# A new order behind the last attention steps: layer-norm statistics, Newton steps, scalings and gates

## The chip, the cores and the metric

The kernel runs on one core of a Trainium2 chip. The metric is the device time in microseconds (us), the median of several runs; less is better. A profile is one execution, in which the hardware profiler records every instruction of each engine. The engines are named as in the profile: PE (matrix multiplication; PEld are its weight loads), DVE (vector), ACT (activation), POOL (GpSimd), SP (which here only issues transfers). Each engine works through its own queue in order; an instruction that waits holds up all behind it on that engine.

## The reference

Sixteen batches `x[b]` of 128 tokens with 512 features go through cross-attention and then through a mixture of experts, each with a layer norm in front and a residual add behind:

```python
x = x + xattn(layernorm(x), ctx, ctx)      # 32 query heads of 16, 8 key heads, 128 context tokens
h = layernorm(x)
scores = sigmoid(h @ gate_weight.T)        # 32 experts in 8 groups
# the best 4 groups by the sum of their two best, then the 8 best experts, weights normed, times 2.5
x = x + sum of the 8 weighted experts(h) + shared expert(h)   # expert: (silu(h w1) * (h w3)) w2
```

All is float32.

## The kernel before

The order of the instructions on PE, DVE, ACT and POOL is written by hand: each engine gets them in the order in which the Python code calls them. SP's transfers stand in the order of their calls too. Waits between engines follow from the data and from buffers that are used again.

Attention (`attention_small`) is a loop over 32 items `(b, i)`, two for each batch. At step n it calls what the dictionary `head` holds for n, then `scores` of item n (PE, then exponentials on ACT, L481), `values` and `add` of item n - 1, `gates` at some steps, what `middle` holds, transposes of the next batch's queries at even steps, transposes of normed rows at some steps, and what `tail` holds.

The parts that matter here:

- `values` (PE L489) fills a PSUM bank, and DVE transposes it out (L499). `add` divides on DVE (L512, L514) and adds to `x[b]` on POOL (L521). For the last batch, 15, each half is added by itself, the second one on DVE.
- `layernorm_stats(b, SECOND)` (DVE L95, L96) takes mean and variance of the rows of `x[b]` after attention. `layernorm_rstd(first, n)` makes 1/sqrt for n batches in Newton steps: twelve tiny instructions on POOL (L102 to L132) or nine on DVE (L102 to L120).
- `gate_rows(b)` scales the rows to the normed `xn` (L136; on DVE or POOL) and has SP write them to `rows` in DRAM (L235). The tile has four buffers.
- `turn_of(b)` ("turn" below): four PE transposes of `xn` (L451) into a bank, which ACT copies to `xall` (L527); for batch 14 DVE copies. `queries(b)` does the same with query rows `xq` (scaled on DVE, L136; copied on ACT, L462).
- `gates(b)`: the gate logits of batches b and b + 1 (PE L540) into a bank, and their transpose by DVE into `logits` (L548).
- All these small products (`values`, turns, queries, gates) share two PSUM banks (`one_bank`, tag `m`) in turn, so each waits until the one before the last is evicted.
- `filler(n)`: n matmuls of the shared expert (PE L285, two records each), which need only batches 0 to 3 and can stand anywhere.

Behind the loop a hand-written tail finishes values, turns 11 to 15 and the gates 8, 10, 12 and 14. Then `route` picks the experts: sigmoid on ACT, a long chain on DVE up to `sel` (L1184) with 21 more fillers on PE, and the counting matmuls (L1192). Then come the slot tables, and the experts, which take the time from about 204 us on. POOL has, behind its part of the tail, a row of memsets (L1014 to L1027) that prepare the experts.

`turned[n]` says which batch is turned at step n, `parts[n]` which gates run at step n (n = 16, 20, 24 and 28 for batches 0, 2, 4 and 6). Statistics of batch b < 14 stand in `tail` at step 2b + 4. POOL's Newton steps run for batches 12 and 13 (columns 28 and 29) in `head` at step 31, and DVE's for 14 and 15 in the tail.

Of the kernel before, what the change touches and what calls it, by code (L numbers as in the profile page):

```python
# [46 lines left out]
def tile_xattn_moe(  # L47
# [15 lines left out]
    nc = tc.nc  # L63
# [29 lines left out]
    def layernorm_stats(b, norm):  # L93
        st = xnp.tile([P, 6], F32, tag="st", name="st")
        nc.vector.bn_stats(st, xs[b])  # L95
        nc.vector.bn_aggr(mv[:, norm[b], :], st)  # L96
# [37 lines left out]
    def normalized(out, of, b, norm, eng=nc.vector):  # L134
        n = norm[b]
        eng.tensor_scalar(out, of, mv[:, n, 0:1], rstd[:, n : n + 1], ALU.subtract, ALU.mult)  # L136
# [19 lines left out]
    SECOND = [*range(12, 15), *range(18, 21), *range(22, 2 * B)]  # L156
# [75 lines left out]
    def gate_rows(b, eng):  # L232
        xn = xnp.tile([P, D], F32, tag="xn2", name="xn2", bufs=4)
        normalized(xn, xs[b], b, SECOND, eng)
        nc.sync.dma_start(rows[ts(b, P), 0:D], xn)  # L235
        xn2[b] = xn
# [67 lines left out]
    def attention_small():  # L304


        with ExitStack() as ph:
# [6 lines left out]
            def one_bank(n=TB):  # L314
                return ps_m.tile([P, TB], F32, tag="m", name="m")[:, 0:n]
# [38 lines left out]
            def keep_warm(n):  # L354
                warm = one_bank(P) if n else None
                for _ in range(n):
                    nc.tensor.matmul(warm, lhsT=wz, rhs=wz, start=True, stop=True)
# [85 lines left out]
            def transposes(of, permuted, then):  # L443
                x = one_bank()
                for k in range(4):
                    if permuted:
                        to = x.rearrange("p (q g s) -> p g q s", g=4, s=HP)[:, k]
                        by = ident.rearrange("p (q s) -> p q s", s=HP)
                    else:
                        to, by = x[:, ts(k, P)], ident  # L450
                    nc.tensor.matmul(  # L451
                        to, lhsT=of[:, k, :], rhs=by, start=True, stop=True, is_transpose=True
                    )
                then(x)

            def queries(b):

                xn = xqs.pop(b).rearrange("p g k d -> p g (k d)")

                def then(x):  # L460
                    qTs[b] = ap2.tile([P, TB], F32, tag="qT", name="qT")
                    (nc.scalar.copy if b > 1 else nc.vector.tensor_copy)(qTs[b], x)  # L462

                return xn, True, then
# [19 lines left out]
            def values(b, i):  # L484
                oT = one_bank()
                for j in range(NJ):
                    p = ps.pop((b, i, j))
                    for q in range(P // HP):
                        nc.tensor.matmul(  # L489
                            oT[q * HP : (q + 1) * HP, ts(j, P)],  # L490
                            lhsT=vas[b // 4 % 2][:, b % 4, 2 * j + i, :],
                            rhs=p[:, ts(q, P)],
                            start=True,
                            stop=True,
                            tile_position=(0, q * HP),
                        )
                if i == 0:
                    os[b] = ap2.tile([P, 2, NJ * G, HP], F32, tag="o", name="o")
                nc.vector.transpose(os[b][:, i].rearrange("p h e -> p (h e)"), oT)  # L499

            def add(b, i, eng=nc.gpsimd):

                if b < B - 1:
                    if i == 0:
                        return
                    both = slice(0, 2)
                else:
                    both = slice(i, i + 1)
                n = both.stop - both.start
                o = os[b][:, both]  # L510
                ri = ap2.tile([P, 2, NJ * G], F32, tag="ri", name="ri")[:, 0:n]
                nc.vector.reciprocal(ri, o[:, :, :, HD])  # L512
                at = ap2.tile([P, 2, NJ * G, HD], F32, tag="at", name="at")[:, 0:n]
                nc.vector.tensor_tensor(  # L514
                    at,
                    o[:, :, :, 0:HD],
                    ri.unsqueeze(3).to_broadcast([P, n, NJ * G, HD]),
                    ALU.mult,
                )
                part = xs[b].rearrange("p (j i e) -> p i j e", i=2, e=G * HD)[:, both]  # L520
                eng.tensor_tensor(  # L521
                    part, part, at.rearrange("p i (j g) d -> p i j (g d)", g=G), ALU.add
                )

            def turn_of(b, copy=nc.scalar.copy):
                def then(x):
                    copy(  # L527
                        xnT[b // 4][:, :, ts(b % 4, P)], x.rearrange("p (k s) -> p k s", s=P)
                    )

                return xn2.pop(b).rearrange("p (k d) -> p k d", d=P), False, then
# [3 lines left out]
            def gates(b):  # L535
                lgT = one_bank(2 * E)
                of = xnT[b // 4].rearrange("p d (n q t) -> p d q n t", n=4, t=E)
                for k in range(ND):
                    for q in range(P // E):
                        nc.tensor.matmul(  # L540
                            lgT[q * E : (q + 1) * E].rearrange("p (n t) -> p n t", t=E),
                            lhsT=gw[:, k, :],
                            rhs=of[:, k, q, b % 4 : b % 4 + 2],
                            start=(k == 0),
                            stop=(k == ND - 1),
                            tile_position=(0, q * E),
                        )
                nc.vector.transpose(logits[:, b : b + 2, :].rearrange("p n e -> p (n e)"), lgT)  # L548
# [3 lines left out]
            head, middle, tail = {}, {}, {}  # L552

            def at(where, n, f, *a):
                where.setdefault(n, []).append((f, a))
# [33 lines left out]

            turned, parts = {}, {}  # L590
            for b in range(14):
                at(tail, 2 * b + 4, layernorm_stats, b, SECOND)
            for n, group in ((10, (8, 7)), (16, (15, 6)), (22, (21, 4)), (27, (25, 3))):
                at(head, n, layernorm_rstd, *group, nc.gpsimd)
            at(head, 31, layernorm_rstd, 28, 2, nc.gpsimd)
            for b in range(11):
                n = min(2 * b + 13, b + 21)
                turned[n] = b
# [10 lines left out]
            for n in range(N):  # L609
                for f, a in head.get(n, ()):  # L610
                    f(*a)

                scores(*items[n])
                if n == 1:
                    transposes(*queries(1))
                if n > 0:
                    values(*items[n - 1])
                    add(*items[n - 1])
                if n in parts:
                    gates(parts[n])  # L620
                for f, a in middle.get(n, ()):
                    f(*a)
                if n % 2 == 0 and 0 < n // 2 < B - 1:
                    transposes(*queries(n // 2 + 1))
                if n in turned:
                    transposes(*turn_of(turned[n]))
                keep_warm(FILL.get(n, 0))
                for f, a in tail.get(n, ()):
                    f(*a)

            gate_rows(12, nc.gpsimd)
            nc.scalar.activation(table, table, AF.Sigmoid)
            gu = ps_sc.tile([P, 2, TB], F32, tag="sc", name="gu")
            banks = iter([gu[:, i] for i in range(2)])
# [3 lines left out]
            def filler(n):  # L640
                for _ in range(n):
                    next(matmuls)

            filler(1)
            values(*items[N - 1])
            add(*items[N - 1], nc.vector)
            transposes(*turn_of(11))
            gate_rows(13, nc.gpsimd)
            gates(8)
            layernorm_stats(14, SECOND)  # L650
            layernorm_stats(15, SECOND)
            layernorm_rstd(SECOND[14], 2)
            filler(1)
            gates(10)
            filler(2)
            transposes(*turn_of(12))
            transposes(*turn_of(13))
            filler(1)
            gates(12)
            gate_rows(15, nc.vector)  # L660
            transposes(*turn_of(15))
            gate_rows(14, nc.vector)
            transposes(*turn_of(14, nc.vector.tensor_copy))
            gates(14)
            filler(3)
# [1356 lines left out]

    pieces = [(k, i) for k in range(NTB) for i in range(NI)]
    left_over = attention_small()
    experts(pieces[1:], in_order, *left_over)
    left = nc.values_load(
# [64 lines left out]
```

## Time and profile before

| | us |
|---|---|
| median of 3 runs | 855.24 (854.67 to 856.40) |
| profiled execution | 855.98 |
| its span, first to last instruction | 853.80 |
| PE busy | 830.5 (97%) |
| DVE busy | 686.4 (80%) |
| ACT busy | 670.9 (79%) |
| POOL busy | 479.3 (56%) |
| first scores matmul of attention | 9.1 |
| last values matmul of attention | 100.7 |
| gates(14) on PE | 112.76 to 113.41 |
| counting matmuls of routing | from 134.14 |

The times in a row of the timeline are the start from the beginning of the span and the length; brackets hold the engine's idle time in front and what ended it. The granted TensorE clock was 0.997 of full speed over the span.

### The profile page before, as it was taken

The page shows a single profiled execution, that of the slowest core. Times are in us where ns is not written, and L with a number is a line of the kernel's source. Part 1 is how long each engine was busy: PE and PEld are TensorE (multiplying, and loading weights), DVE is VectorE, ACT ScalarE, POOL GpSimd, SP SyncE. Part 2 cuts the span into 40 slices and gives each one's busy share as a digit, 9 for nine tenths or more (in the row PEclk, how much of TensorE's full clock was granted, in tenths as well). Part 3 has the DMA queues.
Part 4 walks back from the last instruction along what each step waited for, and adds up shares of the span by engine and source line. Part 5 has one row for each costly group of instructions (what it writes and reads, how often), then busy time and mean ns, then how long its engine had stood idle before and what let it go on. Part 6 is the DMA issues. An engine that isn't in the chain of part 4 may idle for free.

```text
span 853.8 us, 14954 instructions
## 1 busy us (share of the span) xinstructions
PE 830.5 (97%) x4847; PEld 604.2 (71%) x4847; DVE 686.4 (80%) x1660; ACT 670.9 (79%) x1225; POOL 479.3 (56%) x574
## 2 busy tenths in 40 slices
PE   8999989999999999999999999999999999999995
PEld 6555544546676866777787878687878899887763
DVE  7987878849887977988898989898979999986210
ACT  5989622538988896988988989888888999998631
POOL 4597640053445676465548565766657666655453
PEclk9999999999999999999999999999999999999998
DMA  9211113456666798577769696978787978785653
GB/s 282 94 51 64 50 40 128 169 158 197 185 151 150 170 188 240 134 193 174 190 150 234 157 238 157 214 169 199 177 197 187 211 192 188 181 216 126 93 83 50
DMA packets 59879, 137.23 MB, mean 161 GB/s; under 512 B 12168, under 2 KB 16392, under 8 KB 59792
## 3 DMA queue, kind: packets, MB, share of 16 engines
q0 software_dynamic: 32032, 69.25, 41.1%
q1 hardware_dynamic: 27680, 66.81, 23.5%
q8 instruction: 40, 0.66, 0.3%
q14 instruction: 47, 0.39, 0.1%
q10 hardware_dynamic: 80, 0.13, 0.1%
HBM read 96.71 MB, written 46.73 MB: 168 GB/s over the span
## 4 chain that ended last, share of the span: by engine, by line
PE 78%; DVE 7%; ACT 6%; issue 4%; DMA 2%; POOL 2%; POOLq 0%; DVEq 0%; ACTq 0%
PE p L1540 39%; PE y L1781 15%; PE gu L285 6%; PE y L1681 6%; ACT xall L1435 4%; PE y L1334 3%; PE m L489 2%; POOL out_dram L1653 2%; PE sc L471 2%; DMA out_dram<-yp,token 2%; PE gu L1470 2%; PE m L451 2%; DVE o L499 1%; DVE st L95 1%; PE tok L985 1%
## 5 line engine op out<-in xcount | busy, mean ns | idle before, releaser
L1435 ACT COPY xall<-blocks 32x512 f32<-32x512 f32 (+4 forms) x684 | 360.4, 527 | 10.9 <-DVE blocks L1438 0.9
L1653 POOL DMA_INDIRECT out_dram<-yp,token x122 | 201.2, 1649 | 153.6 <-ACT yp L1793 43.2
L1397 POOL DMA_INDIRECT xgs<-rows,token x138 | 153.3, 1111 | 126.1 <-DVE token L997 59.9
L1540 PE MATMUL p<-xall,wup 128*128 128x270 f32 (+27 forms) x720 | 185.9, 393 | 0.0
L1540 PEld LDWEIGHTS p<-xall,wup 128*128 128x128 f32 x720 | 136.7, 190 | 31.6 <-issue 4.7
L1540 PE MATMUL p<-t,s 128*128 128x270 f32 (+27 forms) x480 | 123.6, 394 | 0.0
L1540 PEld LDWEIGHTS p<-t,s 128*128 128x128 f32 x480 | 91.1, 190 | 20.2 <-issue 3.2
L1438 DVE STREAM_TRANSPOSE blocks<-xgs 128x512 f32<-128x512 f32 x138 | 97.0, 703 | 0.0
L1681 PE MATMUL y<-wdn,sa 128*32 128x512 f32 (+2 forms) x288 | 78.7, 596 | 0.0
L1653 POOL DMA_INDIRECT out_dram<-yw,token x28 | 45.1, 1609 | 51.2 <-DMA out_dram<-yw,token 26.1
L481 ACT ACTIVATE p<-sc 128x1024 f32<-128x1024 f32 x64 | 62.0, 1024 | 6.8 <-PE sc L471 6.1
L1550 DVE TENSOR_TENSOR z<-u,p 128x270 f32<-128x270 f32 (+27 forms) x96 | 48.4, 504 | 22.0 <-PE p L1540 21.9
L1540 PE MATMUL p<-xall,s 128*128 128x270 f32 (+27 forms) x240 | 63.5, 395 | 0.8 <-DVE z L1550 0.8
L1540 PE MATMUL p<-t,wup 128*128 128x270 f32 (+27 forms) x240 | 63.8, 396 | 0.0
L285 PE MATMUL gu<-xall,sup 128*128 128x512 f32 x128 | 58.8, 600 | 0.0
L1793 ACT ACTIVATE yp<-yp,wt 128x256 f32<-128x256 f32 (+1 forms) x96 | 54.3, 608 | 3.7 <-DVE yp L1772 2.6
L1772 DVE TENSOR_TENSOR yp<-sdn,y 128x512 f32<-128x512 f32 x72 | 49.1, 682 | 9.7 <-PE y L1781 4.7
L1540 PEld LDWEIGHTS p<-t,wup 128*128 128x128 f32 x240 | 44.9, 190 | 14.7 <-DVE z L1550 3.7
L1540 PEld LDWEIGHTS p<-xall,s 128*128 128x128 f32 x240 | 45.2, 190 | 14.1 <-issue 3.9
L1781 PE MATMUL y<-sup,sa 128*128 128x256 f32 x192 | 49.9, 382 | 3.2 <-ACT sdn L1836 3.0
L1681 PEld LDWEIGHTS y<-wdn,sa 128*32 128x32 f32 (+2 forms) x288 | 28.0, 145 | 30.1 <-issue 28.2
L1781 PE MATMUL y<-wdn,sa 128*128 128x256 f32 x192 | 49.3, 379 | 0.0
(235 smaller groups left out, 1393.1 us busy)
## 6 DMA issues: line engine op xcount, KB each, us to landing
wup<-in_w_dram SPq DMA_DIRECT2D x64, 512.0 KB, 6.3
wdn<-in_w_dram SPq DMA_DIRECT2D x32, 512.0 KB, 5.2
rows<-xn SPq DMA_DIRECT2D x16, 256.0 KB, 2.0
out_dram<-x SPq DMA_DIRECT2D x16, 256.0 KB, 3.1
x<-in_x_dram SPq DMA_DIRECT2D x15, 256.0 KB, 5.2
xgs<-rows,token POOLq DMA_INDIRECT x138, 5.3
out_dram<-yp,token POOLq DMA_INDIRECT x122, 5.5
cTs<-in_cT_dram SPq DMA_DIRECT2D x4, 256.0 KB, 5.1
```

The source lines that it names most:

```text
L285: nc.tensor.matmul(acc, lhsT=sup[:, w, d, ts(i, P)], rhs=xnT[k][:, d, :], start=(d == 0), stop=(d == ND - 1),)
L481: nc.scalar.activation(p, sc, AF.Exp, scale=1.0 / HD**0.5)
L1397: nc.gpsimd.indirect_dma_start(out=t, out_offset=None, in_=rows[:, :], in_offset=bass.IndirectOffsetOnAxis(ap=token[:, j : j + 1], axis=0) ...
L1435: yield on_ACT, 1 + many, lambda dst=dst, of=of, copy=copy: copy(dst, of)
L1438: nc.vector.transpose(blocks[:, j % NB_BUF, :], xgs[:, j % NG_BUF, 0:D])
L1540: nc.tensor.matmul(acc[:, i, 0:h], lhsT=w[:, i, d, :], rhs=x[:, d, :], start=(first and i == d == 0), stop=(i == outs[-1] and d == 1), ski ...
L1550: soon(lambda: nc.vector.tensor_tensor(out_, a, b, ALU.add))
L1653: ins = nc.gpsimd.indirect_dma_start(out=flat, out_offset=bass.IndirectOffsetOnAxis(ap=token2[:, k - 1 : k] if a else token[0:b, j : j + 1 ...
L1681: nc.tensor.matmul(y[c0:c1, :], lhsT=acts_of[k % NA][:, i, col : col + c1 - c0], rhs=wdn[k % NW][:, i, :], start=(i == 0), stop=(i == NI - 1),
L1772: then(lambda: nc.vector.tensor_tensor(to, a, b, op), after)
L1781: nc.tensor.matmul(acc[:, r, :], lhsT=a[:, ts(r, P)], rhs=b, start=(first and r == 0), stop=(r == 1), skip_group_check=not first,)
L1793: lambda r=r, at=at: nc.scalar.activation(to[:, r], of[:, r], AF.Copy, scale=wt[:, at : at + 1]),
```

## The change

It changes only the order of calls.

In the loop: the statistics of batches 12 and 13 stand one step earlier; POOL's Newton steps for 12 and 13 move from step 31 to the head of step 30, which puts them on POOL ahead of the add of batch 14; POOL's scaling of batch 12 moves from behind the loop into step 31, ahead of POOL's half add of batch 15; and `gates` at steps 16, 20, 24 and 28 come behind the transposes of queries instead of in front of them.

In the tail: the statistics of batch 14 stand in front of the last `values`; POOL's scaling of batch 13 stands in front of turn 11; DVE's Newton steps stand behind `gates(10)`; the scalings of 15 and 14 follow at once, in front of `gates(12)`; turn 12 stands in front of the two fillers instead of behind them. On SP, the write of batch 12 to `rows` now precedes that of batch 11.

```diff
@@ attention_small, the plan of the loop
             for b in range(14):
-                at(tail, 2 * b + 4, layernorm_stats, b, SECOND)
+                at(tail, 2 * b + (4 if b < 12 else 3), layernorm_stats, b, SECOND)
             for n, group in ((10, (8, 7)), (16, (15, 6)), (22, (21, 4)), (27, (25, 3))):
                 at(head, n, layernorm_rstd, *group, nc.gpsimd)
-            at(head, 31, layernorm_rstd, 28, 2, nc.gpsimd)
+            at(head, 30, layernorm_rstd, 28, 2, nc.gpsimd)
+            at(head, 31, gate_rows, 12, nc.gpsimd)
@@ the loop
                     add(*items[n - 1])
-                if n in parts:
-                    gates(parts[n])
                 for f, a in middle.get(n, ()):
                     f(*a)
                 if n % 2 == 0 and 0 < n // 2 < B - 1:
                     transposes(*queries(n // 2 + 1))
                 if n in turned:
                     transposes(*turn_of(turned[n]))
+                if n in parts:
+                    gates(parts[n])
                 keep_warm(FILL.get(n, 0))
@@ behind the loop
-            gate_rows(12, nc.gpsimd)
             nc.scalar.activation(table, table, AF.Sigmoid)
...
             filler(1)
+            layernorm_stats(14, SECOND)
             values(*items[N - 1])
             add(*items[N - 1], nc.vector)
+            gate_rows(13, nc.gpsimd)
             transposes(*turn_of(11))
-            gate_rows(13, nc.gpsimd)
             gates(8)
-            layernorm_stats(14, SECOND)
             layernorm_stats(15, SECOND)
-            layernorm_rstd(SECOND[14], 2)
             filler(1)
             gates(10)
+            layernorm_rstd(SECOND[14], 2)
+            gate_rows(15, nc.vector)
+            gate_rows(14, nc.vector)
+            transposes(*turn_of(12))
             filler(2)
-            transposes(*turn_of(12))
             transposes(*turn_of(13))
             filler(1)
             gates(12)
-            gate_rows(15, nc.vector)
             transposes(*turn_of(15))
-            gate_rows(14, nc.vector)
             transposes(*turn_of(14, nc.vector.tensor_copy))
             gates(14)
             filler(3)
```

## The prediction

> **What bounds the kernel now.** I read the busy line of the page first, then the chain that ended last in order of time, then busy time by stretches and the waits around the place of the change, then that place instruction by instruction.
>
> ```profile
> PE 830.5 (97%) x4847; PEld 604.2 (71%) x4847; DVE 686.4 (80%) x1660; ACT 670.9 (79%) x1225; POOL 479.3 (56%) x574
> PE   8999989999999999999999999999999999999995
> ```
>
> PE is busy for 97% of 853.8 us. A new order removes no work, so it can only win PE's idle time. The slices with an 8 are the start and the one from 107 to 128 us. The stretch in question, as busy time by engine (length, PE, PEld, DVE, ACT, POOL):
>
> ```profile
> 101.76:113.34 11.58, 8.38 (x152) 5.00 (x152) 7.24 (x22) 2.13 (x4) 11.50 (x94) 1.00 0.25 93
> ```
>
> Between `gates(8)` (101.76) and the first of the last three fillers (113.34), PE works 8.38 of 11.58 us: 3.20 idle. The clock is at 1.00 here, so no work is slowed, only held. The waits of 96 to 116 us (total us, times, longest) and PE's own rows say by what:
>
> ```profile
> PEld m L451 <- POOL xn L136: 1.7, 2, 1.4
> PE m L451 <- DVE logits L548: 1.2, 1, 1.2
> PE m L451 <- DVE xn L136: 1.1, 1, 1.1
> PE m L540 <- DVE xall L527: 0.9, 1, 0.9
> ```
>
> ```profile
> 107.59 0.63 PE L451 MATMUL m<-ident,xn 128*128 128x128 f32 x4 [1.19 <-DVE logits L548]
> 110.80 1.08 PE L451 MATMUL m<-ident,xn 128*128 128x128 f32 x8 [1.14 <-DVE xn L136]
> 112.76 0.65 PE L540 MATMUL m<-xall,gw 128*32 128x64 f32 x32 [0.88 <-DVE xall L527]
> ```
>
> First, turn(13) at 107.59 waits for a PSUM bank, whose eviction (logits of `gates(10)`) stands on DVE behind two statistics and the nine Newton instructions (105.17 to 107.28), and also for POOL's xn of batch 13 (107.4). Second, turns 15 and 14 wait for xn 15, which DVE does only behind the logits of `gates(12)`. Third, `gates(14)` waits for DVE's copy of turn 14. The three are 3.21 us, all of the idle time. PE's weight loads also wait 0.3 us for POOL's xn 12, at turn(12), behind running fillers. POOL is late because of this order:
>
> ```profile
> 98.61 0.28 POOL L102 TENSOR_SCALAR ve<-mv 128x2 f32<-128x2 f32 x1
> 102.17 0.93 POOL L521 TENSOR_TENSOR x<-x,at 128x256 f32<-128x256 f32 x1
> 103.10 4.31 POOL L136 TENSOR_SCALAR xn<-x,mv,rstd 128x512 f32<-128x512 f32 x2
> ```
>
> **The change, part by part.** Instruction counts stay, so the cost of each step is a matter of place. 0.2% of the time, 1.7 us, is about what a measurement of this kernel can tell from no change.
>
> *Statistics of 12 and 13 a step earlier (DVE).* 0.65 + 0.18 us each. For 12 the add to x ends at 87.18 on POOL; DVE comes free at 88.0 and its next transpose waits for PE until 89.10, so 0.85 us fits into an idle of 1.06. For 13 the add ends at 92.29; behind the transpose of 92.67 to 93.39 the statistics end at about 94.2, then the reduce (0.24) and xn 10 (0.53) end at 95.0, ahead of the next transpose at 95.34. Cost nothing; without that cover 0.3 to 0.8 us, since PE's bank hangs on these transposes.
>
> *Newton of 12 and 13 on POOL ahead of the add of batch 14.* The twelve instructions took 98.61 to 102.22, 3.61 us. They now start at 94.3, where POOL was idle (4.96 us before 97.25), and end at 97.9, or 98.3 if DVE's multiply beside them holds one back as in the 0.55 of an earlier round. The add of 14 (1.28) then ends at 99.2 to 99.6 instead of 98.53, xn 12 (2.16) at 101.4 to 101.8 instead of 105.3, the half add of 15 at 102.3 to 102.7 (before 103.1), xn 13 at 104.5 to 104.9 instead of 107.4. The memsets behind start 2.5 to 2.9 us earlier and end near 112.3 instead of 115.0.
>
> *Statistics of 14 in front of the last transpose on DVE.* This is the one added wait: it needs POOL's add of 14, and the transpose of (15,1), PE's `gates(8)` and the rest are queued behind it. In this place DVE now has no statistics of 13 (0.82), so it comes to the transpose of (15,0) at 98.50 when PE is ready, not at 98.74, and ends its multiply at 99.95. With x 14 ready at 99.2 to 99.6, the statistics run from 99.95 to 100.8, and PE's values end at 100.97. Cost nothing, with 0.15 us to spare.
>
> *DVE's tail.* The statistics of 14 gone from here save 0.8 and the logits of `gates(10)` stand in front of Newton: they are evicted at about 104.35 (PE ends `gates(10)` at 104.0, statistics of 15 end at 104.3). Newton, 2.11 us, ends at 106.7; xn 15 and xn 14 (1.20 for the two) end at 107.9. Before, they ended at 111.1.
>
> *PE's tail.* From 101.76, with durations of the chain: gates(8) 0.63, filler 0.86, gates(10) 0.63, turn(12) 0.59 (xn 12 is ready, its bank since 103.5), two fillers 1.72, turn(13) 0.59 at 106.2 (xn 13 at 104.9, bank at 104.6), filler 0.86, gates(12) 0.63 at 107.65 (ACT's copy of 13 at 107.4), turn(15) 0.59 at 108.3 (xn 15 at 107.3), turn(14) 0.59 at 108.9 (logits(12) evicted at 108.6). Then the copy of turn 14 on DVE and `gates(14)`: this wait of 0.88 stays, nothing fills it. So of 3.20 idle 0.88 is left: 2.32 won. The chain sums to gates(14) ending at 111.0 where it ended at 113.41: 2.4. I take 2.3.
>
> *SP.* Seven writes of xn to `rows` (0.32 to issue, 2.0 to land). That of 12 is now ahead of that of 11 and makes it wait for POOL, to 101.5 where it went at 98.85. It lands by 104, and xn 14, which reuses that buffer, writes at 107.3. Cost nothing.
>
> *Gates behind queries, at four even steps.* Before: gates run in the gap while DVE evicts, then queries wait for the bank:
>
> ```profile
> 66.70 0.66 PE L451 MATMUL m<-ident,xq 128*128 128x128 f32 x4 [0.39 <-DVE o L499]
> ```
>
> After, queries take the free bank at once and gates wait for that same eviction: 0.59 to 0.66 against 0.63 behind it, a difference of 0.0 either way. ACT gets its query copy 0.5 us earlier, but PE bounds there. DVE's logits now stand behind the scaling of a query batch (L136), whose bank the next turn needs:
>
> ```profile
> 67.68 0.24 DVE L548 STREAM_TRANSPOSE logits<-m 128x64 f32<-128x64 f32 x1
> 67.85 1.56 DVE L136 TENSOR_SCALAR xq<-x,mv,rstd 128x512 f32<-128x512 f32 x1
> 67.85 1.28 POOL L521 TENSOR_TENSOR x<-x,at 128x512 f32<-128x512 f32 x1 [0.86 <-DVE at L514]
> ```
>
> That scaling took 1.56 when POOL's add began together with it, 0.53 to 0.59 otherwise. At 1.56 the logits end at 69.5, the turn comes at 69.44: 0.0 to 0.2 us at each of three places. I take 0, because L136 now starts 0.15 us ahead of the add, as at 79.43, where it took 0.59.
>
> *Behind it.* PE runs 24 fillers (20.8 us) to the counting matmuls at 134.2; DVE's routing chain is ready with `sel` at 132.9, 1.3 us early. Both start from gates(14), so the gap stays and all later work moves up by the same 2.3.
>
> **A rule weighed.** The rows: DVE's scaling beside POOL's add took 1.56, DVE's add at 102.56 took 0.83 beside POOL's and ended 0.29 after it, but the pair xn 15, xn 14 took 1.20 beside POOL's memsets. The Trainium skill, "SBUF — State Buffer", section "Who interferes with whom", says that such DVE scalings and GpSimd lock one port pair for a whole instruction, whoever begins first. By it each of the two scalings, now beside the 0.54 us memsets, could wait out one: 1.1 us on DVE, of which 0.75 is covered (xn 14 ends at 107.9, turn(14) would be held from 108.65 on), so 0.3 less gain. The sum goes by the row, 1.20.
>
> **The sum.** The profiled execution took 855.98, 2.18 around its span, and 0.74 above the median of 855.24. 855.98 - 2.3 = 853.7 for such an execution, 852.9 for the median.
>
> **The rivals.** (1) The tail moves, but less: POOL's Newton is held up by DVE's xn 10, multiply and xn 11 (at most 0.53 + 0.69 + 0.55 = 1.8 us), the add of 14 ends at 101, and statistics, transpose and all behind come about 1.1 later: gain 1.2, time 854.0. For it: instructions of 0.43 and 0.55 among those of 0.20. Against: only one per round was so long. Chance 0.10. (2) The gain is won at 113 us and lost behind it, where gathers, sends and weight loads meet otherwise: 0 to 0.7 left, 854.5 to 855.2. For it: the runs of before lie 1.7 apart. Against: PE at 97%, routing moves as a whole. Chance 0.12. (3) Slower: `gates(12)`'s logits and turns 15 and 14 now hang on nine Newton instructions and two scalings in one DVE queue beside POOL's memsets, which Newton did not meet before. If each waits out one memset of 0.54, that is 11 x 0.54 = 5.9, less the 0.75 of slack and the 2.3: 2.9 slower, 858.1. It decides from 3.0 us of added DVE time on. Against: the 1.20 for two scalings beside the same memsets. Chance 0.06.
>
> **How the numbers follow.** The forecast has 0.72; its own range is 852.3 to 853.5 (gains of 1.8 to 2.9). All of it is beyond 1.7 us, so faster 0.72; rivals 1 and 2 lie within 0.2%: 0.22; slower 0.06. The low end: all 3.20 won would be 852.0, with 0.2 for scatter 851.8. The high end takes in rival 1 and the edge of rival 2, 854.6; outside is a part of rival 2 and rival 3.
>
> **What would show it.** Right: gates(14) near 110.4 instead of 112.76, waits on POOL xn and DVE xn gone from turns 12, 13 and 15, the one before gates(14) still near 0.9, the counting matmuls near 131.9. Wrong: a transpose of (15,1) later than 101.1 (rival 1), a DVE stretch from Newton to xn 14 longer than 4.2 us (rival 3), or 2.3 won at the count and a span that is not shorter (rival 2).

## The result and the profile after

The changed kernel takes 861.65 us (855.55 to 863.46), the kernel before beside it 855.23 (854.16 to 857.46): a ratio of 1.0063, 95% interval 1.0048 to 1.0079. By the medians it is slower by 6.4 us, where 2.3 less were forecast; the ratio, which takes all runs in, puts it at 5.4. Of its 20 runs 16 lie between 860.9 and 863.5 and 4 between 855.5 and 856.4; the profiled one is of the many. That execution took 862.0, its span 860.1.

The page first, in the same rows as before:

```profile
PE 834.1 (97%) x4847; PEld 605.4 (70%) x4847; DVE 693.6 (81%) x1660; ACT 670.4 (78%) x1225; POOL 480.0 (56%) x574
PE   8999969999999999999999999999999999999995
PEclk9999979999999999999999999999999999999998
```

DVE has the same 1660 instructions and is busy 7.2 us longer (686.4 before). PE has one slice of 6, the sixth, from 107 to 129 us, and the granted clock falls in it. No other slice of PE or of its clock has changed as much. DVE, then POOL, in the timeline of after around that slice:

```profile
104.79 7.20 DVE L102 TENSOR_SCALAR ve<-mv 128x2 f32<-128x2 f32 x1
112.03 0.17 DVE L104 TENSOR_SCALAR r<-ve 128x2 int32<-128x2 int32 x1
113.64 1.00 DVE L136 TENSOR_SCALAR xn<-x,mv,rstd 128x512 f32<-128x512 f32 x2
...
102.52 2.24 POOL L136 TENSOR_SCALAR xn<-x,mv,rstd 128x512 f32<-128x512 f32 x1
104.70 3.01 POOL L1014 MEMSET xgs<- 128x544 f32 x6
...
110.89 1.07 POOL L1027 MEMSET in_next<- 128x1 f32 x31
```

The first Newton instruction of batches 14 and 15, an addition to 128 x 2 numbers, shows 7.20 us. The shortest DVE instruction of its line takes 0.15. It began 0.09 after POOL's row of 134 memsets (six large ones, then 128 small ones, of which the last group is shown) and ended when the row did (104.70 to 111.96). The rest of Newton and the two scalings take their usual time behind it: 112.03 to 114.64. PE in the timeline, and the stretches (length, then busy time of PE, PEld, DVE, ACT and POOL with instructions, granted clock, DMA share, GB/s):

```profile
107.60 0.65 PE L540 MATMUL m<-xall,gw 128*32 128x64 f32 x32
114.33 1.94 PE L451 MATMUL m<-ident,xn 128*128 128x128 f32 x8 [6.07 <-DVE xn L136]
117.14 1.08 PE L540 MATMUL m<-xall,gw 128*32 128x64 f32 x32 [0.88 <-DVE xall L527]
```

```profile
104.00:112.00 8.00, 4.23 (x46) 2.33 (x46) 7.96 (x4) 1.17 (x2) 7.96 (x136) 0.96 0.11 39
112.00:120.00 8.00, 4.79 (x42) 3.28 (x43) 4.13 (x14) 1.94 (x3) 0.80 (x3) 0.50 0.18 66
```

Turn(15), forecast for 108.3, comes at 114.33 after 6.07 us of waiting for xn 15. Behind this idle time the clock stands at 0.50 for some 8 us. The chain of work that ended last now passes through Newton's first instruction on DVE:

```profile
104.87 7.14 DVE ve L102
...
118.22 22.46 PE gu L285 x48
140.68 0.48 PE count L1192 x16
```

In the same view of before the counting matmuls start at 134.21. The 6.47 us up to there, step by step: the forecast's 2.4 less; turn(15) 6.0 later than forecast; and 2.9 by the lower clock, which is the two turns 1.94 where e1 below shows 1.10 (0.8), `gates(14)` 1.08 for 0.65 (0.4), and the 24 fillers 22.46 for the 20.80 of before (1.7). That makes 6.5. The span is 6.3 longer: the shift passes to the end as a whole.

### The profile page after: what moved, and what is told of

Its sections match the earlier page's. It is cut to its first block, busy times and chain, and to the rows that moved or that the text cites. A ratio compares the mean times of both kernels' runs of the same rounds, so it can differ in the third digit from the quotient of the medians.

```text
span 860.1 us, 14952 instructions
## 1 busy us (share of the span) xinstructions
PE 834.1 (97%) x4847; PEld 605.4 (70%) x4847; DVE 693.6 (81%) x1660; ACT 670.4 (78%) x1225; POOL 480.0 (56%) x574
## 4 chain that ended last, share of the span: by engine, by line
PE 77%; DVE 8%; ACT 5%; issue 4%; POOL 3%; DMA 3%; POOLq 0%; DVEq 0%; ACTq 0%
PE p L1540 38%; PE y L1781 15%; PE gu L285 6%; PE y L1681 5%; PE y L1334 3%; ACT xall L1435 3%; POOL out_dram L1653 2%; PE m L489 2%; PE sc L471 2%; DMA out_dram<-yp,token 2%; PE gu L1470 2%; DVE o L499 1%; DVE st L95 1%; PE m L451 1%; DMA xgs<-rows,token 1%
## 5 line engine op out<-in xcount | busy, mean ns | idle before, releaser
L1781 PE MATMUL y<-sup 128*128 128x256 f32 x192 | 49.3, 379 | 0.0
```

The source lines that it names most:

```text
L1781: nc.tensor.matmul(acc[:, r, :], lhsT=a[:, ts(r, P)], rhs=b, start=(first and r == 0), stop=(r == 1), skip_group_check=not first,)
```

## The experiments

Times are medians; "before" is the kernel before on the same chip: 855.75 (854.25 to 857.37) for e1 to e4; 857.66 (854.5 to 863.57) for e5, e6, e8 and e9; 854.75 (854.2 to 857.97) for e7 and e10 to e12. On the chip of e5, e6, e8 and e9 the kernel before itself fell into two groups (18 runs up to 858.3, 15 from 861.2), so there the ratio to before says little, and the traces and the variants beside each other have to decide.

**e1, the row held back.** One POOL copy that reads xn 14 stands in front of the memsets:

```diff
+    hold = const.tile([P, 1], F32, name="hold")
...
             gate_rows(14, nc.vector)
+            nc.gpsimd.tensor_copy(hold, xn2[14][:, 0:1])
```

> The changed kernel, with POOL held: a copy of one column of xn 14 stands on POOL in front of its memsets, so they start only when DVE has scaled batch 14. Theory P (POOL's unbroken row of memsets shuts DVE's first Newton instruction out for 7.1 us, and PE then runs at a low clock): Newton's first instruction takes 0.2 us, gates(14) starts near 110.4, the clock stays at 1.00, and the predicted 2.3 us come: 852.9. Theory Q (that instruction is late for another reason, a buffer or a semaphore): it takes some 7 us again, 861.6.

852.34 (851.81 to 854.45), ratio 0.9964 [0.9952, 0.9977]. Timeline of e1:

```profile
104.79 0.15 DVE L102 TENSOR_SCALAR ve<-mv 128x2 f32<-128x2 f32 x1
106.54 1.00 DVE L136 TENSOR_SCALAR xn<-x,mv,rstd 128x512 f32<-128x512 f32 x2
...
107.61 0.19 POOL L658 COPY hold<-xn 128x1 f32<-128x1 f32 x1 [2.86 <-DVE xn L136]
...
108.18 1.10 PE L452 MATMUL m<-ident,xn 128*128 128x128 f32 x8
110.16 0.65 PE L541 MATMUL m<-xall,gw 128*32 128x64 f32 x32 [0.87 <-DVE xall L528]
131.54 0.55 PE L1194 MATMUL count<-ones,sel 128*32 128x1 f16 x16
```

The instruction issued at 104.79, as in the changed kernel, takes 0.15. Turn(15) is at 108.18 (108.3 forecast), `gates(14)` at 110.16 (110.4), the count at 131.54 (131.9). The whole forecast comes out once the memsets are out of the way. They now begin at 107.73, and no engine is seen waiting for them up to 140 us.

**e4, POOL's part alone.** The kernel before with the early statistics of 12 and 13 and POOL's new order; DVE's and PE's tail as before:

```diff
-                at(tail, 2 * b + 4, layernorm_stats, b, SECOND)
+                at(tail, 2 * b + (4 if b < 12 else 3), layernorm_stats, b, SECOND)
...
-            at(head, 31, layernorm_rstd, 28, 2, nc.gpsimd)
+            at(head, 30, layernorm_rstd, 28, 2, nc.gpsimd)
+            at(head, 31, gate_rows, 12, nc.gpsimd)
...
-            gate_rows(12, nc.gpsimd)
...
+            gate_rows(13, nc.gpsimd)
             transposes(*turn_of(11))
-            gate_rows(13, nc.gpsimd)
```

> The kernel before, with statistics of 12 and 13 a step earlier and POOL's new order, but the old tail on DVE and PE. The memsets start near 104.7, Newton on DVE comes at 105.2 as before. Theory P: the first Newton instruction is shut out until 112, the logits of gates(10) and all behind are late: gates(14) near 119.5, some 6.5 us later than before, and 3 more by the clock: 861.5 to 865. Theory Q (the cause is the new order on DVE): no long Newton, gain of 0 to 0.5: 855.

865.04 (862.12 to 865.71), ratio 1.0113 [1.0097, 1.0128]: worse than the whole change. Only four runs were taken, and the traced one is the fastest (862.12); the other three, of 864.7 to 865.7, are not explained by it. Timeline of e4:

```profile
104.73 3.01 POOL L1014 MEMSET xgs<- 128x544 f32 x6
...
105.31 0.18 DVE L96 BATCH_NORM_AGGREGATE mv<-st 128x2 f32<-128x6 f32 x1
105.53 6.50 DVE L102 TENSOR_SCALAR ve<-mv 128x2 f32<-128x2 f32 x1
```

The memsets begin ahead of the old tail's Newton too, and Newton's first instruction lasts until the row ends (112.03 and 112.00). The statistics of batch 15 just ahead of it end with their usual 0.18 while the row runs, so not every DVE instruction is held.

**e7, the changed kernel with POOL's old order.** The counterpart: on the changed kernel, POOL's Newton of 12 and 13 goes back behind the add of 14 and its scaling of 12 behind the loop. The early statistics stay.

> The changed kernel with POOL's order of before (Newton of 12 and 13 behind the add of 14), so that the memsets start where they started before, near 107.4, while DVE's and PE's tail and the early statistics stay changed. Theory of the row: Newton's nine (near 104.7 to 106.7) and xn 15 come before the memsets and are not held; xn 14 begins about when the memsets do. If it begins first, turn(13) waits for xn 13 at 107.4 and gates(14) comes near 111.5: gain about 1.2, 854. If it is shut out, it lasts until the memsets end, near 114.7, and the time is 859 to 862. If the changed DVE order itself were the cause, Newton would be long here too.

854.79 (852.9 to 855.59), ratio 0.9985 [0.9972, 0.9998]. Timeline of e7:

```profile
104.26 0.14 DVE L102 TENSOR_SCALAR ve<-mv 128x2 f32<-128x2 f32 x1
...
106.79 0.83 DVE L136 TENSOR_SCALAR xn<-x,mv,rstd 128x512 f32<-128x512 f32 x1
...
105.13 2.21 POOL L136 TENSOR_SCALAR xn<-x,mv,rstd 128x512 f32<-128x512 f32 x1
107.29 1.80 POOL L1014 MEMSET xgs<- 128x544 f32 x3
```

With the same order on DVE as in the changed kernel, Newton is short. The loss therefore comes from POOL's new order; that it comes by way of the memsets, which this order brings forward by 2.6 us, is what e1 and e6 show. Here xn 14 began ahead of the first memset, and that memset waited: it takes 0.82 where one takes 0.54, the first three 1.80 where they would take 1.52. The count, at 132.78, is 1.4 ahead of before, but the times show little of it: the median is that of before, the ratio 0.15% lower, where 1.2 us were expected.

**e6, the row cut short.** The six large memsets go behind the small ones and behind xn 14, so only the row of small ones (some 3.7 us) is left in front of it.

```diff
+            held_by.append(xn2[14])
...
-        for r in range(NG_BUF):
-            nc.gpsimd.memset(xgs[:, r, :], 0.0)
...
+        nc.gpsimd.tensor_copy(hold, held_by[0][:, 0:1])
+        for r in range(NG_BUF):
+            nc.gpsimd.memset(xgs[:, r, :], 0.0)
```

> The changed kernel with the row of memsets cut: the 128 small ones (4.3 us) start at 104.7 as first, the six large ones wait, behind a POOL copy of a column of xn 14, for DVE. Theory P (DVE's instruction gets in where the unbroken row ends): the first Newton instruction ends near 109.1 instead of 112.0, turn(15) comes at 111.5, PE is idle 3.3 us instead of 6, with little or no loss by the clock: 855.5 to 857. If DVE were kept out by large memsets only: 852.5. If by something else than the row: 861.6.

858.15 (854.47 to 859.33), ratio 0.9982 [0.9954, 1.001]. Timeline of e6:

```profile
104.62 3.65 DVE L102 TENSOR_SCALAR ve<-mv 128x2 f32<-128x2 f32 x1
...
107.31 0.94 POOL L1028 MEMSET in_next<- 128x1 f32 x31
```

Half the row, half the wait, and again it ends with the row (108.25). Memsets of 0.09 us, each begun 0.03 after the one before, shut DVE out as well as those of 0.54 do; the size of one instruction does not set the wait. The time is above what I expected, and the clock is what I had underestimated: it is 0.58 from 112 to 120 us although PE waited only 2.52 and 0.88 us. `gates(14)` comes at 112.66, where before it came at 112.76, but it takes 1.08 for 0.65 and the 24 fillers 23.39 for the 20.87 of e1, and the count comes at 136.99, 2.9 later than before.

**e2, other instructions on DVE.** POOL untouched. Newton's first two instructions and the two scalings become forms with two tensors as operands, of the same values:

```diff
-        eng.tensor_scalar(ve, mv[:, first : first + n, 1], EPS, None, ALU.add)
+            eng.scalar_tensor_tensor(ve, var, EPS, var, ALU.add, ALU.max)
...
+            eng.scalar_tensor_tensor(
+                xn, xs[b], mv[:, k, 0:1], rstd[:, k : k + 1].to_broadcast([P, D]),
+                ALU.subtract, ALU.mult,
+            )
```

> The changed kernel, POOL untouched: the four DVE instructions with one tensor operand in the tail (the first two of Newton, and the scalings of 15 and 14) are written in a form with two tensor operands (scalar_tensor_tensor). The memsets stay at 104.7. Theory P in the form 'any DVE work on SBUF is shut out': first Newton instruction long again, 861.6. Theory P in the form 'only the one-operand forms take what the memsets hold': Newton 2 us, scalings 0.7 each (0.3 more in all), gates(14) near 110.6, 853.1. Theory Q: 861.6.

852.84 (852.48 to 854.25), ratio 0.9972 [0.996, 0.9983]. Timeline of e2:

```profile
104.76 0.14 DVE L104 SCALAR_TENSOR_TENSOR ve<-mv 128x2 f32<-128x2 f32 x1
106.50 1.42 DVE L245 SCALAR_TENSOR_TENSOR xn<-x,mv,rstd 128x512 f32<-128x512 f32 x2
...
104.67 3.01 POOL L1030 MEMSET xgs<- 128x544 f32 x6
```

The row begins as in the changed kernel, and DVE works through beside it. A scaling costs 0.75 in this form instead of the 0.55 of e1, which is nothing beside 7. So it is not the memory that POOL fills, nor work that DVE must wait for, but the form of DVE's instruction beside POOL's row. One tensor operand alone is not what is caught: the BATCH_NORM_AGGREGATE of e4 reads one tensor too. Every instruction seen held for the length of the row is a TENSOR_SCALAR.

**e8, Newton alone in that form.** As e2, but the scalings stay as they are.

> The changed kernel with Newton's first two DVE instructions in the form with two tensor operands; the scalings of 15 and 14 keep the one-operand form. Theory P: Newton ends at 106.5, then the scaling of 15 is shut out until the memsets end at 112.0; turn(15) at 112.7 instead of 114.3: 858.5 to 860.5. If a scaling of 128x512 finds its way between memsets as it did before the change (0.75 us at 109.90): near 853.

859.75 (858.12 to 863.49), ratio 1.0005 [0.9977, 1.0032]. Timeline of e8:

```profile
106.64 6.17 DVE L143 TENSOR_SCALAR xn<-x,mv,rstd 128x512 f32<-128x512 f32 x2
```

Newton passes and the next TENSOR_SCALAR is caught: xn 15 takes 5.72 of these 6.17. The first of the kind waits for the rest of the row, whichever it is.

**e5, the clock by itself.** The changed kernel, with 22 matmuls of zeros on PE in front of turn(15):

```diff
+            for _ in range(22):
+                nc.tensor.matmul(wm, lhsT=wz, rhs=wz, start=True, stop=True)
             transposes(*turn_of(15))
```

> The changed kernel with 22 matmuls of zeros (about 0.27 us each, 5.9 in all) on PE in front of turn(15), where PE stood idle for 6 us; nothing waits for their result. DVE's long wait stays. If the low clock behind the idle time (0.50 from 112 to 120 us) is a part of its own of the loss: the clock stays near 1.00, two turns take 1.1 instead of 1.94, gates(14) 0.65 instead of 1.08, 24 fillers 20.8 instead of 22.5: 3.0 us less than the changed kernel, 858.6. If the clock costs nothing beyond the wait: 861.6.

858.95 (858.06 to 860.49), ratio 1.0002 [0.9974, 1.003]. The stretch from 112 to 120 us of e5:

```profile
112.00:120.00 8.00, 6.17 (x59) 3.90 (x58) 5.33 (x19) 2.83 (x4) 0.67 (x3) 1.00 0.18 68
```

The shut-out stays (7.20 for the same instruction), the clock is 1.00 where it was 0.50, the turns take 1.18 for the pair, the count comes at 137.59 where it came at 140.61, and the span is 857.5 where it was 860.1. So 2.6 to 3.0 of the loss is the clock, as the 2.9 read from the trace. The two kernels did not run side by side; the medians, 858.95 against 861.65 and 860.65 (e12), put it at 2.7 and 1.7.

**e3, gates behind queries alone**, on the kernel before.

> The kernel before, with gates behind queries at steps 16, 20, 24 and 28 and nothing else. The prediction put this part at 0 (0.0 to 0.6 us lost): 855.2, at most 855.8. If this part brings the loss: 861.

854.95 (854.41 to 856.19), ratio 0.9995 [0.9986, 1.0004]: no effect that can be measured, as the forecast's 0.

**e9, a filler into the last gap.** e1, with one of the three fillers behind `gates(14)` put in front of it, into the 0.87 us that are left of PE's idle time.

```diff
+            filler(1)
             gates(14)
-            filler(3)
+            filler(2)
```

> POOL held behind xn 14 as in e1, and one of the last three fillers in front of gates(14), where PE waits 0.87 us for DVE's copy. It should fill that wait whole: gates(14) at 110.2 as in e1, the counting matmuls 0.86 earlier, near 130.7; DVE's sel is ready about 130.3 and does not hold them. 0.8 less than e1: 851.5. If sel holds PE: 851.5 to 852.3.

852.28 (850.85 to 853.34), ratio 0.9922 [0.9894, 0.995], a ratio that flatters it, since 15 of the 33 runs of before are the long ones. The count came at 130.73, 0.81 ahead of e1, but the time did not show it across chips. So e1, e9 and the changed kernel ran again together.

**e10 to e12, the three on one chip.**

> The changed kernel with POOL's row of memsets held behind xn 14 once more (the kernel of e1), now on one chip with the next two kernels. Theory (an unbroken row of POOL instructions keeps DVE's waiting instructions out): Newton's first instruction near 0.15 us again, gates(14) near 110.2, the count near 131.5, 852 to 853. If the earlier time was that chip's alone, it lies at the kernel before's time here.

> As e10, with one filler put from behind gates(14) to in front of it (the kernel of e9). By the trace the count comes 0.8 us earlier than in e10; if all behind it moves along, the time is 0.8 less than e10's, 851.5 to 852. If routing's chain on DVE is the later one, it is equal to e10's.

> The changed kernel itself, on one chip with e10 and e11. Theory: Newton's first instruction 7.2 us long, turn(15) near 114.3, 861 to 862, so 9 above e10. If the shut-out is a matter of chance in each execution, a part of its runs lies near 856 as before.

| | us | ratio to before |
|---|---|---|
| e12, the changed kernel | 860.65 (853.57 to 862.13) | 1.0053 [1.0032, 1.0075] |
| e10, with the hold | 851.87 (851.6 to 853.85) | 0.9967 [0.9955, 0.9978] |
| e11, with hold and filler | 851.34 (850.77 to 852.67) | 0.9955 [0.9941, 0.9969] |

In the traces Newton's first instruction takes 7.20 in e12 and 0.14 in e10, and turn(15) comes at 114.32 and 108.04. The hold is worth 8.8 us. The filler is worth 0.5 by the medians (0.8 expected; the intervals overlap), and its count is 0.72 earlier (130.67 against 131.39). e11 beats the kernel before and the changed kernel. e12 has eight runs from 860.1 to 862.1, one of 857.0, and one of 853.57 whose mean clock is 0.997 where the eight have 0.990 to 0.992. That one run lies inside the forecast's range.

## Why the prediction was wrong

**Up to 104.8 us it held**, step by step. POOL's Newton ran at 94.15 to 98.26 (94.3 to 97.9 or 98.3 forecast), the add of 14 ended at 99.49 (99.2 to 99.6), xn 12 at 101.83 (101.4 to 101.8), xn 13 at 104.76 (104.5 to 104.9). The statistics of 14 ran at 99.79 to 100.69 and the transpose of (15,1) began at 100.87, so the added wait cost nothing. The logits of `gates(10)` were out at 104.87 (104.35 forecast), 0.5 late: DVE's multiply and add of the last half took 0.90 and 0.88 beside POOL. The slack took that up. Rival 1, which hung on these steps, did not happen.

**The step that failed is "DVE's tail"**: Newton at 2.11 and the two scalings at 1.20, priced by rows that did not stand as the instructions do now. From Newton's start to the end of xn 14 it took 9.85 us (104.79 to 114.64), of which 7.05 is the wait of one instruction; the prediction had named more than 4.2 as the sign of rival 3. The prediction itself had found that the memsets would start 2.5 to 2.9 us earlier; that brought the whole row in front of Newton (104.70 against 104.79), where before it stood behind it. I then took the 1.20 as proof that scalings get along with memsets. The rows of before show that it was no such proof. The timeline there, DVE and then POOL:

```profile
109.90 1.20 DVE L136 TENSOR_SCALAR xn<-x,mv,rstd 128x512 f32<-128x512 f32 x2
...
109.33 1.04 POOL L1014 MEMSET xgs<- 128x544 f32 x2
110.31 0.38 POOL L1020 MEMSET ranked<- 32x1 f32 x1
110.35 0.35 POOL L1021 MEMSET ranked<- 32x1 f32 x1
```

xn 15 came less than half a microsecond before the last large memset ended, and the small ones behind then show 0.38 and 0.35 where their own time is 0.09: the ends of their records (110.69, 110.70) fit a wait for xn 15, which took 0.75 and ended at 110.65. Two engines shut each other out here, and 1.20 is what it cost when DVE got in. It was the price of one outcome, from one row, and no bound on the other.

**"A rule weighed" named the right rule at the wrong size.** The Trainium skill, "SBUF — State Buffer", section "Who interferes with whom", says that whoever issues first holds the port pair for its whole instruction and the other is fully blocked. By that the estimate was a wait of at most one memset, 0.54. The runs agree that the later one is blocked, and disagree with the length: 7.20, 6.50, 5.72 and 3.65 us, each to the end of POOL's row and not of one instruction. The same section says that a DVE instruction with two SBUF inputs does not contend with a GpSimd instruction that only writes; e2 and e8 agree (0.14 beside the memsets). The paragraph weighed the rule for the two scalings only, but Newton's first two instructions are TENSOR_SCALARs as well, and the first of these was caught.

**Rival 3 had the place and the side right, the wait and its price wrong.** It had the place (nine Newton instructions and two scalings in one queue beside the memsets), but multiplied 0.54 by 11 to get 5.9, 2.9 net, and 858.1. What happened is one wait of 7.05 for the rest of the row, and then no more; and of the eleven instructions only the four TENSOR_SCALARs could have waited, for the other seven took 0.16 each beside the memsets in e8. Its argument against itself, the 1.20, was the wrong row, and its low chance of 0.06 rested on that. The point at which it decides, 3.0 us of added DVE time, leaves out the clock: e6, with 3.5 added, had `gates(14)` about where before had it, and lost 2.9 behind it.

**Missing altogether: the clock.** The forecast's own path left PE idle for at most 0.88 us at a time, so it held the clock at 1.00. Rival 3 would have left it idle for some 5 us and lacked this term. The 6.07 us of waiting brought 0.50 for some 8 us, worth 2.6 (e5) to 2.9 (the rows). The Trainium skill, "TensorE: Matmul & The Clock Gate", "Part 1", gives an idle window of about 3.4 us for that. The 0.50 behind 6.07, and behind 4.14 in e8, agrees. In e6 the clock fell to 0.58 though neither wait was that long (2.52 and 0.88), so a single wait below the window is no assurance.

**Held:** gates behind queries (0 in e3; 66.59 `gates` waits 0.25 where queries waited 0.39), the 0.88 us in front of `gates(14)`, and that what is won or lost at the count passes to the end, within the scatter of single runs (6.47 and 6.3 in after; 1.4 and 0.5 in e7). Rival 2 is thereby out: e1 won 2.6 at the count, and 2.9 and 3.4 in its two medians.

**Left open:** why DVE is kept out for the whole row rather than for one memset, and why it sometimes gets in. Four of 20 and two of 10 runs of the changed kernel escape in whole or in part, to judge by their times, and on one chip the kernel before had 15 of 33 runs at 861.2 to 863.6 with a mean clock (0.989 to 0.993) like that of the changed kernel's long runs (0.990 to 0.992). That its xn 15 is shut out in those is likely but not shown: no profile of such a run, nor of an escape, was taken.

## What to carry to other kernels

When a change makes POOL finish earlier, ask what is queued behind on POOL and which DVE instructions will now meet it: a row of memsets without a gap can cost DVE its whole length, and then PE its clock. Hold such a row behind the work that matters by one instruction that reads its result (8.8 us here), or give DVE the two-operand form (852.84 in e2). And a row that shows two engines sharing a resource gives the price of the outcome that it shows; look at who waited in it before using it as a bound.

## What the runs showed of the hardware

A chain of 134 POOL memsets, the large ones begun 0.49 apart and 0.54 long, the small ones begun 0.03 apart and 0.09 long, so that each begins before the one ahead has ended, kept a DVE TENSOR_SCALAR (128 x 2 or 128 x 512 float32) from finishing until the chain ended: 7.20 us for work of 0.15. Where POOL ran scalings instead of memsets, DVE's TENSOR_SCALARs were held little or not at all (e7: Newton's first two 0.14 and 0.17, xn 14 0.83, after which the first memset waited). Two-operand forms (0.14 to 0.16 in e8), a BATCH_NORM_AGGREGATE (0.18 in e4, at 105.31) and the transpose of the logits out of PSUM (0.25 in the kernel before, at 109.73) were not held by the memsets. The times of one program's runs suggest that the outcome is not the same in each.
